# Two cross-attention layers on one core: layer 2's image scores taken from the bank of the row maxima instead of from a product of their own

## The chip, the cores and the metric

The kernel runs on one core of a Trainium2 chip. The metric is the device time of one execution in microseconds. A core has a matrix engine (TensorE; PE in the profile, with PEld for its weight loads), three engines for element work (VectorE = DVE, ScalarE = ACT, GpSimd = POOL) and a queue engine, SyncE (SP), which issues DMAs and does little else. Each engine runs its own instructions in order. SBUF is the on-chip memory of 128 partitions; PSUM is the small memory that matmuls write, used here in banks of 128 x 512 floats; DRAM lies off the engines and is reached by DMA alone.

## The reference

x is (16 images, 256 positions, 320 channels) and the context (16, 256 tokens, 512). Two layers run one after the other, each with 20 heads of width 16. What matters here is layer 2:

```python
q        = heads(x @ W_q)
k_t, v_t = heads(text @ W_k), heads(text @ W_v)      # text: first 252 tokens
probs_t  = softmax(q · k_t / 4)
text_out = probs_t @ v_t
k_ip, v_ip  = heads(ip @ W_k_ip), heads(ip @ W_v_ip) # ip: last 4 tokens, the "image tokens"
attn_scores = q · k_ip / 4                           # (b, 20 heads, 256, 4)
qsem  = l2norm(probs_t @ text);  sem = qsem · l2norm(ip)
probs_ip = softmax(attn_scores + 0.5 * sem) * spatial_mask
out = (text_out + probs_ip @ v_ip) @ W_out + b_out + x
```

All of it is float32. Layer 1 has the same build with 77 text tokens and 179 image tokens. The attn_scores line of layer 2 is what the change is about: each position has 20 x 4 = 80 of them.

## The kernel before, in words

**Precision.** TensorE multiplies rounded floats, so each operand is split into a rounded part and a rest, and `prod` (L198 to L206) multiplies the parts in three terms. A product of contraction depth 384 is so 9 matmuls, all on line L205.

**Slots.** Five groups of four heads make an image; 16 images make 80 slots a layer. `slot1(k)` (layer 2) is a list of steps written by hand. In slot k, `both1(k, t)` for the two halves t = 0, 1 of the positions makes the transposed scores of group k (L798, tile T) with their exponentials (ACT, L811), and the plain scores of group k+2 (L803, tile S: four heads of 256 columns in one tile of two PSUM banks, one buffer), whose row maxima VectorE takes with one `tensor_reduce` (L804). `maxima1` turns the maxima by matmul (L817), and a DMA puts them under the queries as one more contraction row. `attend1` (L848, L851) multiplies the probabilities with the values; `norm1` (L839, then VectorE's multiplication L840) makes the norm of qsem; `rounded1` (ACT L829, POOL L830) prepares it. `settle1` normalises with VectorE (L893, L896, L897).

**The columns of S.** The keys of an image are written to DRAM and read back in a stacked layout (`ks<-kd`). Keys are 256 columns: 252 text tokens and, from T1 = 252 on, the 4 image tokens' keys, which `keys1` copies in (L466). So each S tile already holds the four image scores of its heads in columns 252 to 255. The reduce L804 reads only the first 252.

**Image scores before.** `open1(b)` prepares image b: it loads x, makes the queries (`queries`, L551, with the splits ACT L559 and DVE L560), and then makes the image scores for itself: `image1` builds a masked key matrix with two VectorE multiplications of 128x384 (L529, from the constant `kmask`), nine matmuls multiply it with the queries (L205, `X<-q,kb`), and one VectorE transpose (L978) brings the result as `si` into the layout of the image softmax: partition 32s + r, eight blocks f, 32 columns, of which 20 (five groups by four tokens) are used. `image_softmax(b)` (L906 to L945) reads `si` on POOL about four slots after the scores were made; its line L945 multiplies the image values (`rs<-vipd`, loaded by SP) by `bmask`, a block mask of 128x384.

**What sets the order.** PE's instructions run in the program's order, pinned. Work besides the slots is in generator tasks (`k1` keys, `t1` tokens, `o1` open1, `i1` image softmax, `c1` close) with due times in slots, stepped by `fill`. `later(d, f)` runs f at d slots after now. In the main loop a scheduler of the framework orders the instructions of VectorE, ScalarE, GpSimd and SyncE; the order of each engine is then fixed in the program. All DMAs go through `dma` (L82) on SP, but for those of the maxima, which ScalarE issues. DMAs of SP rotate over eight completion counters ("lanes"), so that a DMA also waits for the one issued eight earlier. Tiles of one name rotate through a few buffers: three X banks, two T, one P, one S.

**The transition.** Layer 2's weights are split (`weights1`, `weights6`, `weights7`, `weights2`) and its first images opened during layer 1's last slots, at some 600 to 760 us of the profile. `bmask` is loaded at the first `settle1`.

Of the kernel before, what the change touches and what calls it, by code (L numbers as in the profile page):

```python
# [8 lines left out]
F32 = mybir.dt.float32  # L9
FR = mybir.dt.float32r  # L10
# [7 lines left out]
S = 256  # L18
# [3 lines left out]
CP = 384  # L22
E = 512
T0 = 77
NIP = 4
BI = B * NIP
T1 = S - NIP
# [3 lines left out]
NG = H // 4  # L31
# [6 lines left out]
NS = B * NG  # L38
# [10 lines left out]
def xattn2(  # L49
# [31 lines left out]
    def dma(out, in_):  # L81
        nc.sync.dma_start(*(f(ap) if ap.dtype == FR else ap for ap in (out, in_)))  # L82
# [6 lines left out]
    def bank(tag="X"):  # L89
        return ps.tile([128, 512], F32, tag=tag, name=tag, bufs=BANKS[tag])  # L90
# [25 lines left out]
    def const_tile(shape, tag, dtype=F32):  # L116
        return const.tile(shape, dtype, tag=tag, name=tag)
# [23 lines left out]
    def anchor(inst):  # L141
        anchors[inst.ins.engine] = inst
        return inst
# [140 lines left out]

    rn = const_tile([128, BI], "rn")
    kip = const_tile([128, 2, 3, BI], "kip", FR)
    kmask = const_tile([128, 3, 32], "kmask")


    def keys_out(d, m, kst, b=slice(None)):  # L290
# [80 lines left out]
    def weights1():  # L371


        cipn = buf("rawc", [128, 512], bufs=2, name="cipn")[:BI]
        dma(cipn, cip_d)
        yield
        sq = buf("rawc", [128, 512], bufs=2, name="sq")[:BI]
        nc.vector.tensor_mul(sq, cipn, cipn)
        nrm = rn[:BI, 0:1]
        nc.vector.tensor_reduce(nrm, sq, axis=AX.X, op=ALU.add)  # L380
        yield
        nc.scalar.activation(nrm, nrm, AF.Sqrt)
        yield
        nc.vector.tensor_scalar_max(nrm, nrm, 1e-12)
        nc.vector.reciprocal(nrm, nrm)
        dg = buf("rawc", [128, 512], bufs=2, name="dg")[:BI]
        nc.vector.memset(dg[:, BI : BI + 128], 1.0)
        nc.vector.tensor_scalar_mul(dg[:, :BI], ident[:BI, :BI], nrm)
        yield
        rp = bank()  # L390
        mm(rp[:, :BI], dg[:, BI : BI + 128], dg[:, :BI], start=True, stop=True)
        nc.vector.tensor_copy(rn, rp[:, :BI])
        cip = w1["cip"] = buf("kst", [128, 2, 4, BI], FR, bufs=SIZES["KST"], name="cip")
        raw = buf("rawc", [128, 4, BI], bufs=2, name="cipT")
        dma(raw, cipT_d.rearrange("(k p) n -> p k n", p=128))
        yield
        halves(cip[:, 0], cip[:, 1], raw, nc.vector, True)
        yield
# [11 lines left out]
    def weights6():  # L410
        cip = w1["cip"]
        wv = w1["wv"] = buf("wC", [128, 2, 4, H * D + NIP], FR)
        parts = [(wv1_d[k * 128 : (k + 1) * 128], wv[:, 0, k, : H * D], wv[:, 1, k, : H * D]) for k in range(4)]
        yield from in_turn(parts, 0.3, "rawc")
        wvi1 = yield from weights_by_column(wvi1_d, 0.3, "rawc")
        vip = buf("rawc", [128, 512], bufs=2, name="vip")[:BI, :CP]
        for m in range(3):
            ms = slice(m * 128, m * 128 + 128)
            vp = bank()[:BI, :128]
            prod(vp, lambda s, k: cip[:, s, k], lambda s, k: wvi1(s, k, ms), 4)  # L420
            nc.vector.tensor_copy(vip[:, ms], vp)
            yield
        ind1 = buf("M", [2, 2, S], FR, bufs=SIZES["M"], name="ind")
        nc.scalar.activation(ind1, ident[:2, :2].unsqueeze(2).to_broadcast([2, 2, S]), AF.Copy, scale=-1.0)
        w1["ind"] = ind1
        dma(kmask, kmask_d.rearrange("(m p) c -> p m c", p=128))
        dma(vipd, vip)
        for i in range(2):
            v = buf("wD", [128, 2, 640], bufs=2, name="v1t")
            nc.gpsimd.memset(v, 0.0)  # L430
            nc.vector.memset(vcols(v, V1W)[:, 0, :, 16], 1.0)
            nc.vector.tensor_scalar_add(vcols(v, V1W)[:, 1, :, 16], vcols(v, V1W)[:, 1, :, 16], tmask[:, 2:3])
            v1t.append(v)
        yield
# [44 lines left out]
    def tokens1(b):  # L479
# [41 lines left out]
                nc.vector.tensor_add(G[:, 5, :], g[:, S : S + 128], f(G[:, 5, :]))  # L521
            yield
        return V, G

    def image1(b):

        kb = buf("kb", [128, 2, 3, 32, NIP], FR)
        for s in range(2):
            nc.vector.tensor_mul(  # L529
                kb[:, s],  # L530
                f(kip[:, s, :, 4 * b : 4 * b + 4]).unsqueeze(2).to_broadcast([128, 3, 32, NIP]),
                kmask.unsqueeze(3).to_broadcast([128, 3, 32, NIP]),
            )
        return kb.rearrange("p s m c n -> p s m (c n)")

    def split(src, neg, eng, tag):

# [113 lines left out]
    def stacks1(k):  # L651
        b, g = divmod(k - NS, NG)
        n = 2 * SIZES["NR"]
        i = ((NS - SIZES["NR"]) % SIZES["NR"]) * 2 + (k - NS) % n
        Q, K = QK[k] = [x[i // 2 % SIZES["NR"]][:, 2 * (i % 2) : 2 * (i % 2) + 2] for x in (qs, ks)]
        get("k1", b)
        qd = get("o1", b)[0]
        for u in range(2):
            rows = slice(64 * u, 64 * u + XROW)
            hs = slice(4 * g + u, 4 * g + u + 3, 2)  # L660
            if k - NS < n:
                dma(K[64 * u + XROW : 64 * u + KS1], w1["ind"])
            dma(K[rows], stack_rows(kd[1][b][:, :, 0])[:, hs])
            dma(Q[rows], stack_rows(qd)[:, hs])
# [101 lines left out]
    def finish(l, b, hT, resid, extra=None):  # L766
# [14 lines left out]
        yield from project(l, wo[l], hh, evac)  # L781
        return y

    def both1(k, t, between=None):

        a = k + 2 < 2 * NS and QK[k + 2] 
        c = NS <= k < 2 * NS and QK[k]
        if a:
            if t == 0:
                maxes[k + 2] = buf("mn", [128, 4, 4], FR, bufs=2)[:, :2]  # L790
            sp = scores()
        if c:
            st = [bank("T").rearrange("p (h t) -> p h t", h=2) for u in range(2)]
            lo = (0, DUP)[t]
            for j in range(2):
                for u in range(2):
                    rows = slice(64 * u, 64 * u + KS1)
                    mm(st[u][:, j], c[1][rows, j, lo : lo + 128], c[0][rows, j], start=True, stop=True)  # L798
        if a:
            for j in range(2):  # L800
                for u in range(2):
                    rows = slice(64 * u, 64 * u + XROW)
                    mm(sp[:, 2 * u + j], a[0][rows, j, t * 128 : (t + 1) * 128], a[1][rows, j], start=True, stop=True)  # L803
            anchor(nc.vector.tensor_reduce(maxes[k + 2][:, t], sp[:, :, :T1], axis=AX.X, op=ALU.max))  # L804
        if between:
            between()
        if c:
            for u in range(2):
                if t == 0:
                    P[k, u] = buf("P", [128, 2, 2, S], bufs=SIZES["NP"])  # L810
                anchor(nc.scalar.activation(P[k, u][:, t], st[u], AF.Exp, scale=SCALE))  # L811
# [71 lines left out]
    def settle1(b, g, pv):  # L883
        hn = hsn
        if g == 0:
            norms[b] = buf("tmp", [128, NG, 8, 6], bufs=2, name="n1")
        nt = norms[b]
        if "na" not in w1:
            w1["na"], masks = [buf("nt", [128, 2, 8, 32], bufs=2, name="na") for i in range(2)]
            w1["bmask"] = masks.rearrange("p a f c -> p (a f c)")[:, :CP]  # L890
            dma(w1["bmask"], bmask_d)
        na = w1["na"][:, (NG * b + g) % 2]
        nc.vector.transpose(na.rearrange("p f c -> p (f c)"), pv[:, :S])  # L893
        nc.gpsimd.tensor_copy(nt[:, g], na[:, :, 16:22])
        rz = pv[:, S : S + 8]
        nc.vector.reciprocal(rz, na[:, :, 16])  # L896
        nc.vector.tensor_mul(  # L897
            hn[:, g // 2, :, g % 2], na[:, :, 0:16], rz.unsqueeze(2).to_broadcast([128, 8, 16])
        )
        if g == NG - 1:  # L900
            nc.gpsimd.tensor_copy(hn[:, 2, :, 1], hn[:, 2, :, 0])
            later(0.4, lambda: gather(1, b))

    def image_softmax(b, lo=0, hi=NG):

        gs, n = slice(lo, hi), hi - lo  # L906
        nt, si = norms[b][:, gs], get("o1", b)[1]
        pool = nc.gpsimd
        small = lambda n, t: buf(t, [128, NG, 8] + ([n] if n > 1 else []))[:, gs]

# [54 lines left out]
    def open1(b):  # L965
        x = load(x1d[b], "xq")
        yield
        xs = split(x, tmask[:, 5:6], nc.gpsimd, "hq")
        yield
        get("w2")  # L970
        qh, qd = yield from queries(1, xs)

        kb = image1(b)
        yield
        sp = bank()[:, :S]
        prod(sp, lambda s, k: kb[:, s, k], lambda s, k: qh[:, s, k], 3)
        si = buf("si", [128, 8, 32], bufs=3)
        nc.vector.transpose(si.rearrange("p f c -> p (f c)"), sp)  # L978
        yield
        return qd, si  # L980


    results, tasks, clock, delayed = {}, {}, [-99.0], []
# [17 lines left out]
    def get(*key):  # L1001
        while key not in results:
            step(key)
        return results[key]
# [5 lines left out]
    def later(slots, make):  # L1010
        delayed.append((clock[0] + slots, make))
# [196 lines left out]
```

## Time and profile before

| | |
|---|---|
| three runs, us | 1616.49, 1620.4, 1623.62 (median 1620.4) |
| the profiled execution, us | 1612.52 |
| its span in the trace, us | 1610.7 |
| mean granted TensorE clock | 0.977 |
| layer 2, one image in the steady stretch (1034.40 to 1088.70 us) | 54.30 us |

The profile is of one execution, 7.9 us under the median of the runs. It numbers time in us from the start of its span. "Busy" is the time that an engine had an instruction in flight; "idle before" in a row is the time the engine stood waiting ahead of that instruction, and the arrow names who released it. A row of a group gives line, engine, operation, tiles out and in, partitions x elements, count, busy time and mean ns of one.

### The profile page before, as it was taken

What the parts mean: (1) busy time and instruction counts of PE and PEld (TensorE: products, weight loads), DVE (VectorE), ACT (ScalarE), POOL (GpSimd) and SP (SyncE); (2) the same over time, 40 slices, a digit from 0 to 9 for tenths busy, and PEclk for the clock granted to TensorE, in tenths of its full rate; (3) what the DMA queues carried; (4) which work ended last, traced back from release to release, by engine and by line L of the source; (5) the groups of instructions that cost most, each with busy time, mean ns of one, the idle gap of its engine ahead of it and who ended that gap; (6) DMA issues with size and microseconds to landing.
All of it is one profiled execution on the core that took longest, in us unless ns stands there. A gap on an engine that the chain in (4) does not pass through costs nothing.

```text
span 1610.7 us, 36262 instructions
## 1 busy us (share of the span) xinstructions
PE 1518.9 (94%) x13194; PEld 1218.1 (76%) x13194; DVE 1212.2 (75%) x2426; ACT 847.1 (53%) x1861; POOL 1195.7 (74%) x1227
## 2 busy tenths in 40 slices
PE   7899999999999899789999999999999999999996
PEld 6787878787878787577777777777777777777765
DVE  5466777777777678877877787778777887788785
ACT  5344545555555545446656556555655655565562
POOL 3358787878787867777688768876877787778785
PEclk9899999999999899799999999999999999999998
DMA  6767777777677576665424333433343333423301
GB/s 218 214 200 204 206 204 206 205 205 211 199 204 210 170 213 174 162 198 177 149 67 133 114 127 96 131 119 120 96 136 121 107 109 127 130 90 104 110 27 45
DMA packets 235741, 243.05 MB, mean 151 GB/s; under 512 B 19050, under 2 KB 219468, under 8 KB 235564
## 3 DMA queue, kind: packets, MB, share of 16 engines
q1 hardware_dynamic: 233356, 239.44, 49.7%
q8 instruction: 105, 1.72, 0.4%
q10 hardware_dynamic: 2208, 1.30, 0.3%
q14 instruction: 72, 0.59, 0.1%
HBM read 116.78 MB, written 88.18 MB: 127 GB/s over the span
## 4 chain that ended last, share of the span: by engine, by line
PE 63%; DMA 9%; DVE 8%; POOL 8%; ACT 4%; issue 3%; SPq 1%; ACTq 0%; POOLq 0%; DVEq 0%
PE X L205 16%; PE X L839 13%; PE X L551 7%; PE P L732 6%; PE P L848 4%; PE S L675 4%; PE T L798 3%; PE P L851 3%; PE T L699 3%; POOL wt L830 2%; DMA kd<-kst 2%; DMA qs<-qd 2%; DMA qs<-mt 2%; PE S L803 2%; DVE wt L840 1%
## 5 line engine op out<-in xcount | busy, mean ns | idle before, releaser
L705 POOL TENSOR_TENSOR P<-P,rs 128x512 f32<-128x512 f32 x320 | 413.8, 1313 | 149.6 <-ACT P L702 149.5
L830 POOL TENSOR_TENSOR wt<-P,ctb 128x512 f32<-128x512 f32 x320 | 419.0, 1324 | 95.0 <-ACT ctb L829 93.6
L839 PE MATMUL X<-ctb,gm 128*128 128x512 f32 x1120 | 329.9, 412 | 0.7 <-DVE wt L840 0.4
L702 ACT ACTIVATE P<-T 128x512 f32<-128x512 f32 x320 | 176.0, 595 | 211.8 <-PE T L699 113.9
L839 PEld LDWEIGHTS X<-ctb,gm 128*128 128x128 f32 x1120 | 188.9, 188 | 69.2 <-issue 15.2
L840 DVE TENSOR_TENSOR wt<-X,wt 128x512 f32<-128x512 f32 x320 | 218.4, 683 | 18.9 <-PE X L839 13.4
L804 DVE TENSOR_REDUCE mn<-S 128x4 fp32r<-128x1008 f32 x160 | 191.7, 1198 | 49.1 <-PE S L803 48.9
L829 ACT ACTIVATE ctb<-P 128x512 fp32r<-128x512 f32 x320 | 195.1, 630 | 40.1 <-PE X L839 35.8
L811 ACT ACTIVATE P<-T 128x512 f32<-128x512 f32 x320 | 173.1, 593 | 68.9 <-PE P L848 53.8
L677 DVE TENSOR_REDUCE mn<-S 128x4 fp32r<-128x716 f32 x160 | 142.5, 891 | 0.0
L699 PE MATMUL T<-qs,ks 127*128 127x256 f32 x640 | 111.7, 294 | 21.9 <-DVE tmp L749 9.8
L732 PE MATMUL P<-P,vr 128*32 128x256 f32 x1920 | 128.7, 404 | 0.9 <-DVE mx L604 0.9
L675 PE MATMUL S<-ks,qs 125*128 125x256 f32 x640 | 118.4, 309 | 4.9 <-DVE mn L677 2.8
L675 PEld LDWEIGHTS S<-ks,qs 125*128 125x128 f32 x640 | 89.2, 196 | 41.3 <-issue 36.2
L551 PE MATMUL X<-ho,wF 128*128 128x256 f32 x768 | 113.2, 291 | 6.5 <-DVE ho L541 3.0
L551 PE MATMUL X<-hq,wE 128*128 128x256 f32 x768 | 109.7, 286 | 7.1 <-ACT hq L540 3.2
L917 POOL TENSOR_TENSOR r<-u,rs 128x40 f32<-128x40 f32 (+2 forms) x17 | 108.7, 6394 | 7.4 <-DVE u L914 7.2
L551 PEld LDWEIGHTS X<-ho,wF 128*128 128x128 f32 x768 | 103.7, 195 | 12.7 <-DVE ho L541 4.6
L699 PEld LDWEIGHTS T<-qs,ks 127*128 127x128 f32 x640 | 92.5, 197 | 27.2 <-DVE tmp L749 11.2
L551 PEld LDWEIGHTS X<-hq,wE 128*128 128x128 f32 x768 | 102.3, 193 | 11.3 <-ACT hq L540 3.7
L205 PE MATMUL X<-cta,wA 128*128 128x252 f32 (+1 forms) x720 | 101.1, 287 | 8.9 <-ACT wA L147 5.8
L205 PEld LDWEIGHTS X<-cta,wA 128*128 128x128 f32 x720 | 94.3, 193 | 15.1 <-ACT wA L147 6.1
(207 smaller groups left out, 2854.9 us busy)
## 6 DMA issues: line engine op xcount, KB each, us to landing
qd<-q SPq DMA_DIRECT2D x96, 384.0 KB
qs<-tph SPq DMA_DIRECT2D x64, 308.0 KB
kd<-kst SPq DMA_DIRECT2D x73, 256.0 KB
rawc<-in_cT_dram SPq DMA_DIRECT2D x60, 256.0 KB
qs<-qd SPq DMA_DIRECT2D x80, 192.0 KB
ks<-kd SPq DMA_DIRECT2D x80, 192.0 KB
ks<-kd SPq DMA_DIRECT2D x160, 96.0 KB
qs<-qd SPq DMA_DIRECT2D x160, 96.0 KB
```

The lines of the kernel that those rows point to most:

```text
L205: last = mm(out, lhs(a, k), rhs(b, k), start=i == 0, stop=i == len(terms) - 1)
L551: mm(pp, w(s, k, slice(m * 128, (m + 1) * 128)), a[:, t], start=i == 0, stop=i == len(terms) - 1)
L675: mm(sp[:, h], Q[: XROW + T0, h, t * 128 : (t + 1) * 128], K[: XROW + T0, h], start=True, stop=True)
L699: mm(st[p][:, j], K[:KS0, 2 * p + j, t * 128 : (t + 1) * 128], Q[:KS0, 2 * p + j], start=True, stop=True)
L702: exp = anchor(nc.scalar.activation(pt, st[p], AF.Exp, scale=SCALE))
L705: anchor(nc.gpsimd.tensor_mul(pt, pt, rs[:, t : t + 1].to_broadcast([128, 2, S])))
L732: mm(pv[32 * s : 32 * s + 32, o : o + S], v[:, vt, h : h + 32], P[k, s // 2][:, t, s % 2], start=vt < 2, stop=vt != 1,)
L804: anchor(nc.vector.tensor_reduce(maxes[k + 2][:, t], sp[:, :, :T1], axis=AX.X, op=ALU.max))
L829: nc.scalar.activation(R[k, u][:, t], P[k, u][:, t], AF.Copy, scale=0.5)
L830: anchor(nc.gpsimd.tensor_sub(W[k, u][:, t], P[k, u][:, t], f(R[k, u][:, t])))
L839: mm(yp, gm[:, gb], R[k, u][:, kt], start=i == 0, stop=i == len(blocks[n]) - 1)
L840: nc.vector.tensor_mul(W[k, u][:, n], yp, W[k, u][:, n])
```

## The change

Layer 2's image scores are no longer computed by a product of their own. Behind each row maximum (L804) VectorE copies columns 252 to 255 of the same S tile, for four heads, into a tile `sq` of SBUF. After an image's last half, `sq` goes to DRAM (`sd`), and 0.6 slots later eight DMAs read it back into `si` in the softmax's layout, in pieces of 20 floats. `si` has 20 columns instead of 32. The key matrix `image1`, its constant `kmask`, its nine matmuls and the transpose go. `bmask` is copied DRAM to DRAM (`hop`) where the first weights of layer 2 are emitted and loaded from there into the buffers that `image1` used; it is no longer loaded at the first `settle1`. In the order of SP's program, the copy to `hop` stands where `kmask` was loaded, as the 19th DMA of the kernel.

```diff
-    kmask = const_tile([128, 3, 32], "kmask")
...
         dma(cipn, cip_d)
+        hop = w1["hop"] = dram.tile([128, CP], F32, name="hop")
+        dma(hop, bmask_d)
...
-        dma(kmask, kmask_d.rearrange("(m p) c -> p m c", p=128))
+        w1["bmask"] = f(buf("kb", [128, CP], FR, name="bmask"))
+        dma(w1["bmask"], w1["hop"])
...
-    def image1(b):
-
-        kb = buf("kb", [128, 2, 3, 32, NIP], FR)
-        for s in range(2):
-            nc.vector.tensor_mul(
-                kb[:, s],
-                f(kip[:, s, :, 4 * b : 4 * b + 4]).unsqueeze(2).to_broadcast([128, 3, 32, NIP]),
-                kmask.unsqueeze(3).to_broadcast([128, 3, 32, NIP]),
-            )
-        return kb.rearrange("p s m c n -> p s m (c n)")
...
+    def image_scores(k, t, sp):
+
+        b, g = divmod(k - NS, NG)
+        if (g, t) == (0, 0):
+            image[b] = buf("sq", [128, 2, 4, NG * NIP], bufs=2)
+        sq = image[b]
+        nc.vector.tensor_copy(sq[:, t, :, NIP * g : NIP * (g + 1)], sp[:, :, T1:S])
+        if (g, t) == (NG - 1, 1):
+            sd = dram.tile([128, 2, 4, NG * NIP], F32, tag="sd", name="sd", bufs=2)
+            dma(sd, sq)
+            later(0.6, lambda: image_out(b, sd))
+
+    def image_out(b, sd):
+
+        si = image[b] = buf("si", [128, 8, NG * NIP], bufs=3)
+        for s in range(4):
+            for u in range(2):
+                dma(si[32 * s : 32 * s + 32, 4 * u : 4 * u + 4], sd[:, u, 2 * (s % 2) + s // 2].rearrange("(a r) x -> r a x", r=32))
...
             anchor(nc.vector.tensor_reduce(maxes[k + 2][:, t], sp[:, :, :T1], axis=AX.X, op=ALU.max))
+            image_scores(k + 2, t, sp)
...
-            w1["na"], masks = [buf("nt", [128, 2, 8, 32], bufs=2, name="na") for i in range(2)]
-            w1["bmask"] = masks.rearrange("p a f c -> p (a f c)")[:, :CP]
-            dma(w1["bmask"], bmask_d)
+            w1["na"] = buf("nt", [128, 2, 8, 32], bufs=2, name="na")
...
-        nt, si = norms[b][:, gs], get("o1", b)[1]
+        nt, si = norms[b][:, gs], image[b]
...
-        kb = image1(b)
-        yield
-        sp = bank()[:, :S]
-        prod(sp, lambda s, k: kb[:, s, k], lambda s, k: qh[:, s, k], 3)
-        si = buf("si", [128, 8, 32], bufs=3)
-        nc.vector.transpose(si.rearrange("p f c -> p (f c)"), sp)
-        yield
-        return qd, si
+        return qd
```

More of the change, by code (lines that the diff above doesn't have):

```diff
@@ L656, in stacks1 @@
         get("k1", b)
-        qd = get("o1", b)[0]
+        qd = get("o1", b)
         for u in range(2):
@@ L782, in finish @@
         return y
+    image = {}
+    def image_scores(k, t, sp):
[13 more added lines that the diff above has]
+                dma(si[32 * s : 32 * s + 32, 4 * u : 4 * u + 4], sd[:, u, 2 * (s % 2) + s // 2].rearrange("(a r) x -> r a x", r=32))
     def both1(k, t, between=None):
```

## The prediction, on record before the changed kernel ran

> **What bounds the kernel now.** I read the page's busy line and chain first, then the table by windows, then what PE waited for, and only then single instructions.
>
> ```profile
> span 1610.7 us, 36262 instructions
> ...
> PE 1518.9 (94%) x13194; PEld 1218.1 (76%) x13194; DVE 1212.2 (75%) x2426; ACT 847.1 (53%) x1861; POOL 1195.7 (74%) x1227
> ...
> PE 63%; DMA 9%; DVE 8%; POOL 8%; ACT 4%; issue 3%; SPq 1%; ACTq 0%; POOLq 0%; DVEq 0%
> ```
>
> The averages hide stages. The table by windows has, after the stretch and its length: busy us (count) of PE, PEld, DVE, ACT and POOL, the granted clock, the DMA share and GB/s.
>
> ```profile
> 640.00:700.00 60.00, 45.07 (x395) 34.62 (x395) 47.27 (x96) 28.02 (x63) 43.84 (x45) 0.83 0.67 181
> 700.00:755.00 55.00, 48.42 (x432) 40.17 (x433) 42.07 (x78) 29.43 (x65) 43.50 (x51) 1.00 0.61 188
> ...
> 1034.40:1088.70 54.30, 53.63 (x461) 41.13 (x460) 43.02 (x80) 30.80 (x67) 41.29 (x45) 1.00 0.36 117
> 1088.70:1143.10 54.40, 53.70 (x462) 41.09 (x460) 43.09 (x80) 30.95 (x68) 41.47 (x45) 1.00 0.38 117
> ```
>
> The last two rows are two images of layer 2's steady stretch: PE is busy in 53.6 of 54.3 us, idle in 0.7; DVE has 11.3 us free, POOL 13. So there a matmul less is time less, unless something else comes late; and a small operation more on DVE costs only where PE waits for DVE. The first two rows are the transition: PE is idle in 14.9 + 6.6 = 21.5 us, DVE often the cause. PE's waits over six steady images (us in total, times, longest):
>
> ```profile
> PE X L954 <- DVE wt L840: 2.5, 6, 0.4
> PE X L520 <- DVE gm L516: 1.1, 6, 0.2
> ```
>
> Two waits an image, both on DVE, 0.4 and 0.2 us. These are the places to which new DVE work can reach.
>
> **Term 1: the product goes.** The timeline of PE around one image's product, and the same place in a slot without one; first its group over the whole trace:
>
> ```profile
> L205 PE MATMUL X<-q,kb 128*128 128x256 f32 x144 | 20.8, 288 | 0.2
> ```
> ```profile
> 1044.62 0.70 PE L954 MATMUL X<-rs,rs 128*128 128x256 f32 x2 [0.43 <-DVE wt L840]
> ...
> 1045.85 0.28 PE L817 MATMUL X<-ident_r,mn 128*4 128x128 f32 x2
> 1046.06 0.50 PE L798 MATMUL T<-qs,ks 50*128 50x256 f32 x4
> ...
> 1067.34 0.28 PE L817 MATMUL X<-ident_r,mn 128*4 128x128 f32 x2
> 1067.46 1.27 PE L205 MATMUL X<-q,kb 128*128 128x256 f32 x9
> 1068.66 0.51 PE L798 MATMUL T<-qs,ks 50*128 50x256 f32 x4
> ```
>
> From L817 to L798 it takes 1068.66 - 1067.34 = 1.32 us with the product and 1046.06 - 1045.85 = 0.21 without: 1.11 us an image, with no idle before any of the three. The program order of the changed kernel has the same PE instructions without these 144, so 16 x 1.11 = **-17.8 us**. The two images whose product lies in the transition, where PE has idle time anyway, may give less; the range takes that in.
>
> **Term 2: the copies.** Ten per image, 160 in all, each 128x16 from PSUM. In the changed program each stands directly behind its reduce on DVE. No such copy is in the trace. The nearest rows in size, with the two operations that go:
>
> ```profile
> L529 DVE TENSOR_TENSOR kb<-kip,kmask 128x384 fp32r<-128x384 f32 x32 | 35.6, 1115 | 5.9 <-PE X L205 5.9
> ...
> L746 DVE RECIPROCAL P<-nt 128x16 f32<-128x16 f32 x80 | 19.7, 246 | 0.0
> ...
> L747 DVE TENSOR_TENSOR P<-P,mk 128x8 f32<-128x8 f32 x80 | 13.4, 168 | 1.6
> L978 DVE STREAM_TRANSPOSE si<-X 128x256 f32<-128x256 f32 x16 | 7.0, 437 | 0.5 <-PE X L205 0.5
> ```
>
> 0.17 us (8 elements) and 0.25 us (16, a reciprocal) bound it; I take 0.2, between. Ten are 2.0 us an image, and 2 x 1.115 + 0.437 = 2.67 us go, so DVE's load falls by 0.7 us an image. The sum isn't the point, though: the removed work stood in one place, the new is spread over ten. Which of the ten can PE feel? The one in the chain to the 0.43 us wait, on DVE:
>
> ```profile
> 1041.87 0.65 DVE L840 TENSOR_TENSOR wt<-X,wt 128x512 f32<-128x512 f32 x1
> 1042.44 0.41 DVE L560 TENSOR_TENSOR q<-X,q 128x256 fp32r<-128x256 f32 x1
> 1042.78 1.19 DVE L804 TENSOR_REDUCE mn<-S 128x4 fp32r<-128x1008 f32 x1
> 1043.89 0.67 DVE L840 TENSOR_TENSOR wt<-X,wt 128x512 f32<-128x512 f32 x1
> ```
>
> DVE works without a gap from 1041.87 to 1044.56, and PE's L954 starts at 1044.62, when this L840 has freed its bank. A copy behind the reduce of 1042.78 makes L954 late by its whole length: 0.2 us. Queued behind it on DVE are L840 and L955, behind L954 on PE everything. The other nine stand before gaps of DVE's or on banks that PE needs later; the only other wait in the list, L516's, has one more reduce ahead. For the nine together I take 0.1 (bounds 0 and 1.8). So +0.3 us an image; with 14 images in the steady stretch **+4.2 us** (bounds 0 and 28).
>
> In a sentence of its own: the Trainium skill, "VectorE: DVE Perf Modes", section "The TRN2 errata — SBUF-src ops pay a fixed extra latency per instruction", gives a VectorE operation from PSUM 120 cycles plus one per element at 0.96 GHz, and warns that many small tiles pay the fixed part each, which speaks against ten small copies; the estimate by it is 136 / 0.96 = 142 ns, and term 2 would be 3.0 us. The trace agrees on the reduce (1128 cycles are 1.175 us, the row has 1.19), and no run here shows a copy yet.
>
> The S tile is freed later by the copy too. It is a single buffer, so the next L803 waits for it. Of the ten in the image of 1034 us, the tightest pair is a reduce on DVE and the next L803 on PE:
>
> ```profile
> 1049.10 1.20 DVE L804 TENSOR_REDUCE mn<-S 128x4 fp32r<-128x1008 f32 x1
> ```
> ```profile
> 1052.19 0.40 PE L803 MATMUL S<-ks,qs 48*128 48x256 f32 x4
> ```
>
> 1052.19 - 1050.30 = 1.89 us are free, nine copies long. Cost nothing; if that cover were gone, 0.2 us for each slot half.
>
> **Term 3: the way through DRAM.** Nine DMAs an image on SP. The timeline of SP, and the last reduce of the image on DVE:
>
> ```profile
> 1079.57 0.43 SPq L82 DMA_DIRECT2D qs<-qd  x1
> 1091.34 0.39 SPq L82 DMA_DIRECT2D out_dram<-xc  x1
> 1095.06 0.38 SPq L82 DMA_DIRECT2D xc<-x1d  x1
> ...
> 1096.06 0.44 SPq L82 DMA_DIRECT2D rawc<-in_cT_dram  x1
> 1099.76 0.53 SPq L82 DMA_DIRECT2D rs<-vipd  x1
> ```
> ```profile
> 1086.38 1.20 DVE L804 TENSOR_REDUCE mn<-S 128x4 fp32r<-128x1008 f32 x1
> ```
>
> SP stands idle from 1080.0 to 1091.3. The last copy ends at about 1086.38 + 1.20 + 0.2 = 1087.8, so sd is issued then, in the gap. The first si waits at SP's head until sd has landed: at most 3.7 us, what xc, which needs out_dram's transfer done, waited behind it (1091.34 to 1095.06). The new order is sd, four si, out_dram, two si, xq, si, xc, si, rawc, rs. At some 0.48 us an issue out_dram goes at 1093.4 at the latest, xc 3.7 us behind it at 1097.1, rawc at about 1098.1. rs waits for PE until 1099.76 in any case: 1.2 us of margin. And si is read by POOL some four slots later, 40 us. So **0**. If the cover were gone, rs is what is late, and VectorE's L945 with it (the third rival).
>
> **Term 4: the transition.** On the chain of waits, on PE and on DVE there stand:
>
> ```profile
> 641.59 1.36 DVE kb L529 x2
> ```
> ```profile
> 753.65 0.22 PE L817 MATMUL X<-ident_r,mn 128*4 128x128 f32 x1 [0.85 <-DVE mn L804]
> ```
> ```profile
> 756.46 0.94 DVE L945 TENSOR_TENSOR rs<-rs,nt 128x384 f32<-128x384 f32 x1 [1.68 <-DMA nt<-in_bmask_dram]
> ```
>
> The L529 at 641.59 is in the chain that ended last: up to -1.36. PE's 0.85 is a reduce that DVE comes to late, after two L529; with the early bmask L945's 1.68 us of idle go as well, but no PE wait hangs on those in the rows. Other products of this stretch give a little. Late next is the split of weights on the same engine. I take **-3** (bounds -8 and +2: new copies, and 18 DMAs more for the first two images on a crowded SP).
>
> **Term 5: the start.** kmask goes, hop comes at its place among the first loads:
>
> ```profile
> 12.10 0.43 SPq L82 DMA_DIRECT2D kmask<-in_kmask_dram  x1
> ```
> ```profile
> GB/s 218 214 200 204 206 204 206 205 205 211 199 204 210 170 213 174 162 198 177 149 67 133 114 127 96 131 119 120 96 136 121 107 109 127 130 90 104 110 27 45
> ```
>
> 192 KB instead of 48 KB; 144 KB at the first slice's 218 GB/s are 0.7 us, twice that if read and write both count, nothing if the loads behind it aren't late. I take **+0.4** (0 to 1.4).
>
> **The sum.** -17.8 + 4.2 + 0 - 3 + 0.4 = -16.2 us. Against the profiled execution, 1612.5 us (span 1610.7 and 1.8 around it), that is 1596.3. That execution is 7.9 us below the median of the runs, 1620.4; against the median the forecast is 1620.4 - 16.2 = **1604**.
>
> **The rivals.**
> *Bigger gain.* No copy is felt and the transition gives 8: -17.8 - 8 = -25.8, 1595. For it: DVE has less to do in sum. Against: the L954 chain above has no gap.
> *The copies eat the gain.* DVE works in order, and PE at 99% has no idle time to take up delays. If half of the ten copies are felt, 1.0 us an image in place of 0.3, the loss is 0.7 x 14 = 9.8: 1614, within what counts as no change; if all ten, 1.7 x 14 = 23.8: 1628. Break-even is at about seven of ten. Against it stand the 1.89 us on the S tile and the two short waits.
> *rs comes late: slower.* It is one mechanism: SP issues in order and the nine DMAs stand ahead of rs<-vipd. The price can be read one image earlier, on SP and on DVE:
>
> ```profile
> 1045.35 0.53 SPq L82 DMA_DIRECT2D rs<-vipd  x1
> ```
> ```profile
> 1050.21 0.80 DVE L945 TENSOR_TENSOR rs<-rs,nt 128x384 f32<-128x384 f32 x1
> ```
>
> L945 comes 4.9 us after the issue, without a wait. If rs is issued late by more than this leaves, DVE stands there, behind it the L840 that frees PE's banks, and each us is a us of PE. It decides from about 1.2 us of such lateness an image (16.2 / 14); at 3 us the loss is 42, 1646; at 2 us, 28, **1632**. For it speaks that one si is 128 pieces of 80 bytes, and that with eight lanes a slow si holds up what is issued eight later: rawc waits for the fourth si. Against it: the margin of 1.2 us by upper bounds, and 5 us between that si and rawc. By the Trainium skill, "DMA: Bandwidth & Descriptors", section "Specifications", a transfer needs 512 B for line rate; 80 B are below it, which makes this rival likelier; no run here shows such an si yet.
> *It isn't what it says.* Were copies moved away from their reduces, the S tile would be held; the program order shows none moved.
>
> **How the numbers follow.** About 0.5%, 8 us, is what a measurement of this kernel can tell from no change; the borders are 1612 and 1628. The forecast and its near surroundings (1595 to 1612) get 0.63, the bigger gain beyond that 0.08, the eaten gain 0.15, the late rs 0.14. The first two are faster, 0.71; the third is the same, 0.15; the fourth slower, 0.14. The range of 1593 to 1618 holds the first, most of the second and the milder half of the eaten gain, about 0.8.
>
> **What would show each step.** Right: in the steady windows an image of about 53.5 us (54.35 - 1.11 + 0.3), PE idle about 1.0 us of it; a copy row of 0.14 to 0.25 us; PE's wait at L954 about 0.6 us; S waits none; sd issued in SP's gap, rs right after PE's L954; no idle of DVE ahead of L945. Wrong: a new PE wait S L803 <- DVE of the copy; PE waits at L839 or L798 that weren't there; L945 with "<-DMA rs" before it; an image of 54 us or more.

## The result, and the profile after

The changed kernel runs in 1594.39 us (median of four, 1590.43 to 1596.61) against 1618.7 us (median of four) for the kernel before: ratio 0.9849, 95% interval 0.9829 to 0.9869. That is 24 us less; 16 were forecast (1604), and the time lies within the stated range of 1593 to 1618, near its lower end. Its profiled execution took 1596.61 us, 15.9 less than the profiled one of before. Which of the two differences is the change's will have to be settled first.

Line numbers move in the changed kernel: L810 and L815 are the old L798 and L803 (T and S scores), L816 the reduce, L783 the new copy, L830 the old L817, L852/L853 the norm's L839/L840, L965 the old L954, L956 the old L945, L518/L522 the old L516/L520, and L690, L723 and L740 the old L699, L732 and L749. In the other kernels below they move again; the text names the old line beside the new one. The page:

```profile
span 1594.8 us, 36348 instructions
...
PE 1507.8 (95%) x13050; PEld 1206.7 (76%) x13050; DVE 1192.8 (75%) x2538; ACT 848.6 (53%) x1861; POOL 1192.1 (75%) x1227
...
PE 67%; DMA 8%; DVE 8%; POOL 6%; ACT 4%; issue 3%; SPq 2%; ACTq 0%; POOLq 0%; DVEq 0%
```

PE has 144 matmuls less; DVE has 112 instructions more (160 copies, 48 gone) and yet is busy 19 us less. The table by windows, in the transition and in one steady image (columns as in the prediction):

```profile
640.00:700.00 60.00, 46.82 (x408) 36.03 (x408) 48.41 (x99) 28.71 (x64) 46.45 (x49) 0.84 0.77 209
700.00:755.00 55.00, 50.57 (x416) 41.11 (x417) 38.27 (x77) 29.40 (x65) 41.07 (x48) 0.92 0.56 171
...
1019.80:1073.30 53.50, 52.72 (x457) 40.16 (x457) 41.38 (x86) 31.01 (x66) 41.40 (x45) 1.00 0.39 121
```

In the steady window DVE is busy 41.4 us where it was 43.0. The length of an image is read from one matmul that comes once in each, the last pair of L954 (now L965). In the kernel before, on PE, nine images apart:

```profile
935.93 0.70 PE L954 MATMUL X<-rs,rs 128*128 128x256 f32 x2 [0.41 <-DVE wt L840]
```
```profile
1424.98 0.70 PE L954 MATMUL X<-rs,rs 128*128 128x256 f32 x2 [0.40 <-DVE wt L840]
```

and in the changed one, the same nine images:

```profile
931.86 0.70 PE L965 MATMUL X<-rs,rs 128*128 128x256 f32 x2 [0.54 <-DVE wt L853]
```
```profile
1411.89 0.70 PE L965 MATMUL X<-rs,rs 128*128 128x256 f32 x2 [0.54 <-DVE wt L853]
```

489.05 / 9 = 54.34 us before, 480.03 / 9 = 53.34 after: **1.00 us an image**. PE's waits over six images of the changed kernel are the same two, and the first has grown:

```profile
PE X L965 <- DVE wt L853: 3.3, 6, 0.6
PE X L522 <- DVE gm L518: 1.1, 6, 0.2
```

The copy's group, and then the chain to that wait on DVE's timeline:

```profile
L783 DVE COPY sq<-S 128x16 f32<-128x16 f32 x160 | 25.9, 162 | 0.0
```
```profile
1089.90 1.19 DVE L816 TENSOR_REDUCE mn<-S 128x4 fp32r<-128x1008 f32 x1
1091.02 0.16 DVE L783 COPY sq<-S 128x16 f32<-128x16 f32 x1
1091.10 0.67 DVE L853 TENSOR_TENSOR wt<-X,wt 128x512 f32<-128x512 f32 x1
```

A copy is 162 ns long, but the next instruction starts 80 ns after it: the row's duration overlaps its neighbour's. On SP's timeline the way through DRAM:

```profile
1080.37 0.34 SPq L82 DMA_DIRECT2D sd<-sq  x1
1081.98 1.73 SPq L82 DMA_DIRECT2D si<-sd  x4
...
1088.68 0.39 SPq L82 DMA_DIRECT2D rawc<-in_cT_dram  x1
1092.56 0.53 SPq L82 DMA_DIRECT2D rs<-vipd  x1
```

sd has landed at the latest 1.6 us after its issue (the first si goes out then); rawc's issue is done at 1089.1, and rs goes out another 3.5 us later, 0.73 us after the start of PE's L965 at 1091.83. Lastly the transition, before on DVE and on PE, then after on both:

```profile
641.50 2.35 DVE L529 TENSOR_TENSOR kb<-kip,kmask 128x384 fp32r<-128x384 f32 x2
...
644.24 1.45 DVE L148 TENSOR_TENSOR wC<-rawc,wC 128x320 fp32r<-128x320 f32 x1
...
646.71 0.41 DVE L749 TENSOR_TENSOR tmp<-nt,P 128x256 f32<-128x256 f32 x1
```
```profile
647.17 0.80 PE L699 MATMUL T<-qs,ks 127*128 127x256 f32 x2 [3.87 <-DVE tmp L749]
```
```profile
643.60 0.42 DVE L740 TENSOR_TENSOR tmp<-nt,P 128x256 f32<-128x256 f32 x1
```
```profile
644.18 1.05 PE L690 MATMUL T<-qs,ks 127*128 127x256 f32 x4
```

Before, the pair L529 stood ahead of L749, which by the row releases the last two of PE's four L699 and L732 behind them; a cast of 1.45 us stood between as well, and PE waited 3.87 us. After, L740 (the old L749) stands ahead of that cast, and PE's four L690 run without a break.

### The profile page after: what moved, and what is told of

It is laid out like the page before. It is cut to its first block, busy times and chain, and to the rows that moved or that the text cites. A ratio compares the mean times of both kernels' runs of the same rounds, so it can differ in the third digit from the quotient of the medians.

```text
span 1594.8 us, 36348 instructions
## 1 busy us (share of the span) xinstructions
PE 1507.8 (95%) x13050; PEld 1206.7 (76%) x13050; DVE 1192.8 (75%) x2538; ACT 848.6 (53%) x1861; POOL 1192.1 (75%) x1227
## 4 chain that ended last, share of the span: by engine, by line
PE 67%; DMA 8%; DVE 8%; POOL 6%; ACT 4%; issue 3%; SPq 2%; ACTq 0%; POOLq 0%; DVEq 0%
PE X L205 16%; PE X L852 14%; PE X L542 7%; PE P L723 6%; PE P L861 4%; PE S L666 4%; PE T L810 4%; PE P L864 4%; PE T L690 3%; DMA qs<-qd 2%; DMA kd<-kst 2%; POOL wt L843 2%; PE S L815 2%; SPq L82 2%; DMA qs<-mt 1%
## 5 line engine op out<-in xcount | busy, mean ns | idle before, releaser
L852 PE MATMUL X<-ctb,gm 128*128 128x512 f32 x1120 | 330.0, 412 | 0.5 <-DVE wt L853 0.3
L852 PEld LDWEIGHTS X<-ctb,gm 128*128 128x128 f32 x1120 | 189.1, 188 | 68.1 <-issue 21.4
L853 DVE TENSOR_TENSOR wt<-X,wt 128x512 f32<-128x512 f32 x320 | 218.2, 683 | 20.8 <-PE X L852 12.7
L842 ACT ACTIVATE ctb<-P 128x512 fp32r<-128x512 f32 x320 | 195.1, 630 | 41.4 <-PE X L852 38.5
L816 DVE TENSOR_REDUCE mn<-S 128x4 fp32r<-128x1008 f32 x160 | 191.7, 1198 | 25.7 <-PE S L815 25.0
L723 PE MATMUL P<-P,vr 128*32 128x256 f32 x1920 | 132.2, 411 | 1.7 <-DVE mx L595 1.6
L690 PE MATMUL T<-qs,ks 127*128 127x256 f32 x640 | 110.9, 294 | 18.1 <-DMA qs<-mt 9.1
L690 PEld LDWEIGHTS T<-qs,ks 127*128 127x128 f32 x640 | 92.0, 197 | 22.9 <-DVE tmp L740 7.3
```

What stands on the lines that cost most here:

```text
L690: mm(st[p][:, j], K[:KS0, 2 * p + j, t * 128 : (t + 1) * 128], Q[:KS0, 2 * p + j], start=True, stop=True)
L723: mm(pv[32 * s : 32 * s + 32, o : o + S], v[:, vt, h : h + 32], P[k, s // 2][:, t, s % 2], start=vt < 2, stop=vt != 1,)
L842: nc.scalar.activation(R[k, u][:, t], P[k, u][:, t], AF.Copy, scale=0.5)
L852: mm(yp, gm[:, gb], R[k, u][:, kt], start=i == 0, stop=i == len(blocks[n]) - 1)
L853: nc.vector.tensor_mul(W[k, u][:, n], yp, W[k, u][:, n])
```

## The experiments

The theory after the first result: PE's 1.11 us an image are the gain; one copy in ten is felt; in the transition the pair of multiplications of image 0 costs PE more than itself. The rivals: copies that pile up, an SP queue that makes rs late, and a gain that comes from the mask's new place. And first, whether 24 or 16 us are to be explained.

**How far do executions of one program differ?** `before_again` is the kernel before, `after_again` the changed one, both unchanged.

> The kernel before, unchanged, against itself, for what differs between executions of one program. The changed kernel's trace is 15.9 us shorter in its span, its median 24.3 us; layer 1, whose instructions are the same, drifts by -3.9 to +1.9 us between the two traces. Theory 'scatter' (the change is worth about 16 us and the rest is chance of execution): ratio 1.000 within 0.003, and a second profile whose layer 1 (100 to 640 us) differs from the first by several us. Theory 'the change is worth 24 us': the ratio is 1.000 as well, but the profiles of both kernels, taken again, lie about 24 us apart.

> The changed kernel, unchanged, timed in five rounds. Theory 'PE work less the exposed copy' (16 x 1.11 us less, some 0.15 us an image more, some us in the transition): ratio 0.988 to 0.991 (about 15 to 19 us). Theory 'worth 24 us': 0.985 or less, and the profile has places outside the steady images of layer 2 where some 8 us go.

The kernel before against itself: 1.0001 (0.9987 to 1.0015). The changed one: 0.986 (0.9841 to 0.9878), that is 20 to 26 us less. The second profile of the kernel before has a span of 1621.7 us, 11 more than the first, without one instruction changed. The table by windows of its two profiles, first and second, shows where:

```profile
100.00:640.00 540.00, 512.09 (x4706) 439.38 (x4706) 398.17 (x894) 270.42 (x626) 428.62 (x408) 0.98 0.69 199
640.00:760.00 120.00, 98.49 (x881) 78.35 (x882) 92.64 (x179) 59.07 (x131) 89.33 (x97) 0.91 0.64 184
```
```profile
100.00:640.00 540.00, 514.53 (x4675) 441.94 (x4677) 397.31 (x889) 270.95 (x624) 426.34 (x407) 0.97 0.68 197
640.00:760.00 120.00, 96.11 (x839) 75.36 (x832) 87.53 (x168) 53.67 (x121) 86.51 (x94) 0.89 0.61 174
```

The granted clock (the third number from the end) is 0.01 to 0.02 lower there, and fewer matmuls fit into the same stretch. So the first profile of before was a lucky execution: the 15.9 us between the two profiles understate the change, and the 24 of the first medians lie within the second interval too. Steady images, at a clock of 1.00, don't have this scatter: the same nine images of the second profile take 54.35 us each.

**The product, and the copies by themselves.** `no_product` leaves out layer 2's image scores (the softmax reads zeros) with all that made them; `copies_only` keeps the old path and adds the 160 copies, whose tile nobody reads.

```diff
 no_product
+        w1["si"] = buf("si", [128, 8, 32], bufs=1)
+        nc.gpsimd.memset(w1["si"], 0.0)
...
-        kb = image1(b)
         yield
-        sp = bank()[:, :S]
-        prod(sp, lambda s, k: kb[:, s, k], lambda s, k: qh[:, s, k], 3)
-        si = buf("si", [128, 8, 32], bufs=3)
-        nc.vector.transpose(si.rearrange("p f c -> p (f c)"), sp)
+        si = w1["si"]
 copies_only
+    def image_scores(sp):
+
+        nc.vector.tensor_copy(buf("sq", [128, 4, NIP], bufs=2), sp[:, :, T1:S])
...
             anchor(nc.vector.tensor_reduce(maxes[k + 2][:, t], sp[:, :, :T1], axis=AX.X, op=ALU.max))
+            image_scores(sp)
```

> Left out: the image scores of layer 2 (the softmax reads zeros); no key matrix, no product, no transpose, no copies, no DMAs for them; the block mask is loaded late as before. Theory 'the product's PE time is the gain': 16 x 1.11 = 17.8 us and up to 3 in the transition, ratio 0.987 to 0.989; it beats the changed kernel by the exposed copies alone, 2 us. Rival 'a good part of the gain is the early block mask or the transition': this kernel gains 8 us less than the changed one.

> The old path is kept whole; behind each row maximum the copy of the four columns is added, into a small tile that nobody reads (no DMAs). Theory 'one copy in ten is felt': 0.13 to 0.2 us an image, 2 to 3 us in all, ratio 1.001 to 1.002; PE's wait at L954 grows from 0.42 to about 0.55 us, no new wait at S. Rival 'the copies eat': half of the ten are felt, 0.8 us an image, 12 us, ratio 1.007 to 1.008; all ten, 26 us, 1.016.

`copies_only`: 1.0027 (1.001 to 1.0043), between the two theories. Its steady images tell them apart; on PE, eleven images apart:

```profile
863.57 1.27 PE L205 MATMUL X<-q,kb 128*128 128x256 f32 x9
```
```profile
1462.27 1.28 PE L205 MATMUL X<-q,kb 128*128 128x256 f32 x9
```

598.70 / 11 = 54.43 us, 0.09 more than before, at a granted clock of 1.00. So ten copies cost about 0.1 us an image here; half of them felt would be 0.4 by the measured 80 ns. The rest of the 0.27%, some 3 us, isn't in the steady images, and where it is wasn't found.

`no_product`: 0.9895 (0.9877 to 0.9913), 17 us less, *fewer* than the changed kernel. That spoke for the rival that the early mask brings the rest.

**Is it the mask?** `bmask_late` is the changed kernel with the mask loaded at the first settle1 and no hop; `no_product_early` is `no_product` with hop and the early mask, without kmask.

```diff
 bmask_late
-        hop = w1["hop"] = dram.tile([128, CP], F32, name="hop")
-        dma(hop, bmask_d)
...
-        w1["bmask"] = f(buf("kb", [128, CP], FR, name="bmask"))
-        dma(w1["bmask"], w1["hop"])
...
-            w1["na"] = buf("nt", [128, 2, 8, 32], bufs=2, name="na")
+            w1["na"], masks = [buf("nt", [128, 2, 8, 32], bufs=2, name="na") for i in range(2)]
+            w1["bmask"] = masks.rearrange("p a f c -> p (a f c)")[:, :CP]
+            dma(w1["bmask"], bmask_d)
```

> The changed kernel with the block mask loaded late again, at the first settle1, and no copy to DRAM at the start. Theory 'the early mask is worth nothing, or costs 0.4 us': same as the changed kernel, ratio 0.985 to 0.987. Rival 'the rest of the gain is the early mask' (the kernel without product, mask late, gained 17 us, the changed one 23, and its trace is about 5 us behind in the transition): ratio 0.989 to 0.990, and the stretch of 625 to 765 us is some 5 us longer than in the changed kernel.

> Left out: the image scores of layer 2, as before, but the block mask is loaded early as in the changed kernel and kmask is gone. Rival 'the early mask is worth some 6 us': ratio 0.984 to 0.985, 2 us better than the changed kernel. Theory 'the mask is worth nothing': 0.989 to 0.990 as with the late mask.

`bmask_late` 0.9835 (0.9808 to 0.9862), `no_product_early` 0.9835 (0.9805 to 0.9866); both medians, 1594.48 and 1595.02, are the changed kernel's. The mask's new place is worth nothing measurable to the changed kernel, and the rival falls. Why `no_product` alone gained 17 can be read in part from its trace: in the transition it has two PE waits, of 2.68 and 2.46 us, that `no_product_early` hasn't. The second hangs on the late mask, on DVE and PE (L947, L806 and L819 are the old L945, L804 and L817):

```profile
756.61 0.81 DVE L947 TENSOR_TENSOR rs<-rs,nt 128x384 f32<-128x384 f32 x1 [1.87 <-DMA nt<-in_bmask_dram]
757.34 1.20 DVE L806 TENSOR_REDUCE mn<-S 128x4 fp32r<-128x1008 f32 x1
```
```profile
758.59 0.22 PE L819 MATMUL X<-ident_r,mn 128*4 128x128 f32 x1 [2.46 <-DVE mn L806]
```

VectorE's order in this kernel has the product with the mask ahead of a row maximum that PE needs; in the kernel before and in `bmask_late` it stands behind that maximum, and the mask's lateness doesn't reach PE. So a late mask costs where the order puts it ahead of such work. The first wait, for a cast of ScalarE's, and the rest of the difference stay open. The image without product or copies, from `no_product_early`, the same nine images on PE (L945 and L833 are the old L954 and L840):

```profile
931.80 0.70 PE L945 MATMUL X<-rs,rs 128*128 128x256 f32 x2 [0.41 <-DVE wt L833]
```
```profile
1410.53 0.70 PE L945 MATMUL X<-rs,rs 128*128 128x256 f32 x2 [0.40 <-DVE wt L833]
```

478.73 / 9 = 53.19 us: the product, with its work on VectorE, is worth 54.34 - 53.19 = 1.15 us an image, and the copies of the changed kernel cost 53.34 - 53.19 = 0.15. Of this the longer wait at L965 is 0.13 (3.3 us in place of 2.5 over six images).

**Twice the copies.** `copies_twice` adds a second copy of the same columns behind each first.

```diff
         nc.vector.tensor_copy(sq[:, t, :, NIP * g : NIP * (g + 1)], sp[:, :, T1:S])
+        nc.vector.tensor_copy(buf("sq2", [128, 4, NIP], bufs=2), sp[:, :, T1:S])
```

> The changed kernel with a second copy of the same columns behind each first, into a tile that nobody reads. The first copy costs 0.12 to 0.15 us an image (trace: 1.11 - 1.0). Theory 'one copy in ten is felt': another 0.15 us an image, 2 to 2.5 us in all, ratio to the kernel before up by 0.001 to 0.002; PE's wait at L965 grows by one copy, to 0.7 us. Rival 'the copies begin to pile up': over 0.6 us an image more, 9 us.

0.9888 (0.9859 to 0.9916), 7 us more than the changed kernel, and 0.71 us an image ((1468.68 - 874.17) / 11 = 54.05, from the two rows below) where 0.15 was expected: the rival's number. But it isn't ten copies adding up. PE's waits, and the first and last L966 (the changed kernel's L965):

```profile
PE X L522 <- DVE gm L518: 6.7, 6, 1.1
PE X L966 <- DVE wt L854: 2.0, 6, 0.3
```
```profile
874.17 0.70 PE L966 MATMUL X<-rs,rs 128*128 128x256 f32 x2 [0.33 <-DVE wt L854]
```
```profile
1468.68 0.70 PE L966 MATMUL X<-rs,rs 128*128 128x256 f32 x2 [0.33 <-DVE wt L854]
```

L966 waits even less, by 0.2 us; what grew is one wait, at L522, from 0.2 to 1.1 us. The two together make the 0.71. DVE and POOL ahead of L518, from one timeline of both:

```profile
1078.35 0.68 DVE L854 TENSOR_TENSOR wt<-X,wt 128x512 f32<-128x512 f32 x1
...
1078.95 1.57 DVE L533 SCALAR_TENSOR_TENSOR hq<-hq,tmask,xq 128x256 fp32r<-128x256 f32 x1
1078.95 3.94 POOL L844 TENSOR_TENSOR wt<-P,ctb 128x512 f32<-128x512 f32 x3
```

and the same place in the changed kernel:

```profile
1080.86 0.47 DVE L533 SCALAR_TENSOR_TENSOR hq<-hq,tmask,xq 128x256 fp32r<-128x256 f32 x1
1081.15 1.34 POOL L843 TENSOR_TENSOR wt<-P,ctb 128x512 f32<-128x512 f32 x1 [0.72 <-ACT ctb L842]
```

The scheduler, with the longer VectorE program, has changed the order around L533, which now starts together with a POOL operation and takes 1.57 us; in the changed kernel it starts while POOL stands idle and takes 0.47. The group rows over six images, changed kernel and `copies_twice`:

```profile
L533 DVE SCALAR_TENSOR_TENSOR hq<-hq,tmask,xq 128x256 fp32r<-128x256 f32 x6 | 2.8, 473 | 0.0
```
```profile
L533 DVE SCALAR_TENSOR_TENSOR hq<-hq,tmask,xq 128x256 fp32r<-128x256 f32 x6 | 9.5, 1576 | 0.0
```

The added copies change the order, and L533 takes 1.1 us more in the new one, ahead of the L518 that PE waits for. This is read from the traces; no run has the second copies in the old order. By the Trainium skill, "SBUF — State Buffer", section "Who interferes with whom", a VectorE instruction with two SBUF inputs contends with a GpSimd instruction that reads SBUF, and the one that comes second waits for the other's end; the trace agrees, the 1.1 us more being nearly one POOL operation (1.3).

**The way through DRAM.** `si_twice` and `si_thrice` issue each load of si two and three times.

```diff
             for u in range(2):
+                for _ in range(2):
                     dma(si[32 * s : 32 * s + 32, 4 * u : 4 * u + 4], sd[:, u, 2 * (s % 2) + s // 2].rearrange("(a r) x -> r a x", r=32))
```

> The changed kernel with each of the eight loads of si issued twice on SP, so that eight more DMAs of 128 pieces of 80 bytes stand ahead of rs<-vipd in each image. Theory 'the way through DRAM is hidden': at 0.45 us an issue 3.6 us more on SP; if the margin ahead of rs is about 1 to 4 us, the steady image stays within 0.1 us, at most L945's row gets a short wait. Rival 'SP's queue is near its limit': rs lands some 2 us late, L945's row of VectorE shows a wait for it and the image grows by up to 2 us, ratio 1.00.

> The changed kernel with each of the eight loads of si issued three times: 16 more DMAs an image ahead of rs<-vipd. With each issued twice rs went out 1.95 us after the PE matmul it waits for, in place of 0.73, and L945 of the kernel before (rs times the mask, on VectorE) still started 5.6 us after that matmul, as in the changed kernel: the slack took it. Eight more issues at 0.57 us make rs 4.5 us later still, issued 6.5 us after the matmul; with some 2 to 3 us to land it comes at 8.5 to 9.5. Theory 'rs late stalls VectorE and PE': L945 shows a wait of 3 to 4 us an image, the image grows by 2.5 to 3.5 us, 35 to 50 us in all, ratio 1.007 to 1.017. Rival 'nothing hangs on it': the steady image stays within 0.2 us of the changed kernel's, and the slower way that the prediction named was never near.

0.9832 (0.9805 to 0.9858) and 0.9841 (0.9813 to 0.9869): nothing. In `si_twice` the margin is used up, as SP's and PE's timelines show:

```profile
1082.08 5.10 SPq L82 DMA_DIRECT2D si<-sd  x9
1087.28 0.39 SPq L82 DMA_DIRECT2D rawc<-in_cT_dram  x1
1087.77 1.13 SPq L82 DMA_DIRECT2D rs<-vipd  x1
```
```profile
1085.82 0.70 PE L966 MATMUL X<-rs,rs 128*128 128x256 f32 x2 [0.56 <-DVE wt L854]
```

rs follows rawc without a pause, 1.95 us after the matmul instead of 0.73, but VectorE's product with it still starts 5.6 us after that matmul (at 1091.42), as in the changed kernel (1097.42, matmul at 1091.83). In `si_thrice` the scheduler put rs ahead of the last seven si, so rs wasn't later still; the point from which a late rs costs was not reached by either run, and its price wasn't measured.

**The transition.** `keys_first` is the changed kernel with the two multiplications of image 0 alone kept, unread, with kmask's load and the late mask.

```diff
...
         qh, qd = yield from queries(1, xs)
 
+        if b == 0:
+            image1(b)
+        yield
         return qd
```

> The changed kernel with the two multiplications of 128x384 kept for image 0 alone (their result is not read), kmask loaded at its old place and the block mask loaded late. In the kernel before, this pair stands on VectorE at 641.5 us ahead of the operation that frees PE's bank, and PE waits 3.87 us there; in all kernels without it the stretch of 635 to 645 us is 3.6 to 5.3 us shorter. Theory 'the pair makes that wait': PE's wait of about 4 us is back at the same place, 2.4 us of DVE costing more than themselves since a cast behind them slows as well; 625 to 765 us longer by some 4 us, ratio up by 0.0025. Rival 'the order around it has changed anyway': no such wait, ratio as the changed kernel's. And the first 300 us, shorter by 1 to 3 us in kernels without kmask: longer again if kmask's load is the cause, not if chance of the clock is.

0.9903 (0.9882 to 0.9924), 1602.28 us, some 8 us above `bmask_late`. PE's wait is back where it was (L699 and L749 have the same numbers here as in the kernel before):

```profile
649.56 0.80 PE L699 MATMUL T<-qs,ks 127*128 127x256 f32 x2 [4.10 <-DVE tmp L749]
```

Matched instruction by instruction with the first profile of before, PE's stretch from 635 to 645 us is 3.6 to 5.3 us shorter in the kernels without the pair (4.65 in the changed kernel's first profile) and 0.6 shorter in this one, about what the second profile of before shows too (0.7); its steady images are the changed kernel's. So two instructions of 1.2 us each on VectorE, in one place, cost PE about 4 us. That is half of the 8 us; the other half isn't shown. Over the first 300 us, matched in the same way, the five kernels with kmask's load lie 0 to 1.9 us above that first profile, this one 0.2, and the nine without it from 3.7 below to 1.5 above; the means are 0.9 above and 1.3 below. The two overlap, the granted clock scatters there, and no run takes kmask's load alone away: what kmask and hop do at the start stays open.

One more wait of the transition is gone, the 0.85 us ahead of L817 at 753.65 that the prediction lists. In the changed kernel, on PE:

```profile
752.70 0.28 PE L830 MATMUL X<-ident_r,mn 128*4 128x128 f32 x2
```

Matched in the same way, the stretch from 750 to 755 us is 1.07 us shorter in every kernel without the product, `keys_first` among them, but for `no_product` with its wait for the mask, and the same within 0.1 us in the second profile of before and in `copies_only`.

**Can the felt copy be moved?** `copy_behind_norm` orders each copy behind the next norm multiplication; `copies_act` puts it on ScalarE.

```diff
 copy_behind_norm
-            image_scores(k + 2, t, sp)
+            pending.append((k + 2, t, sp))
...
-        nc.vector.tensor_mul(W[k, u][:, n], yp, W[k, u][:, n])
+        flush(nc.vector.tensor_mul(W[k, u][:, n], yp, W[k, u][:, n]))
 copies_act
-        nc.vector.tensor_copy(sq[:, t, :, NIP * g : NIP * (g + 1)], sp[:, :, T1:S])
+        nc.scalar.copy(sq[:, t, :, NIP * g : NIP * (g + 1)], sp[:, :, T1:S])
```

> The changed kernel with each copy ordered on VectorE behind the next multiplication L840 of the kernel before (it frees the bank PE waits for), not directly behind its reduce. Theory 'the felt copy is the one in the chain to L954': PE's wait there is 0.42 us again in place of 0.55, the steady image some 0.12 us shorter, 2 us in all, ratio 0.001 below the changed kernel. Rival 'the S tile is then held too long': the reduce's tile is held about 0.7 us longer of 1.9 free; PE waits at S, the image gets longer.

> The changed kernel with the ten copies of an image on ScalarE. ScalarE is busy in 31 of 54 us an image and holds the exponentials and the casts that PE's operands come from. Theory 'only the chain on VectorE feels a copy': 0.12 us an image less, ratio 0.001 below the changed kernel. Rival 'a copy in ScalarE's order waits for the S tile ahead of exponentials, or they for it': PE waits at T or at the ScalarE casts appear, ratio above the changed kernel by 0.003 or more.

`copy_behind_norm`: 0.9907 (0.9882 to 0.9931), 8 us worse than the changed kernel; my theory lost to the rival. The wait at L954 is gone, and one at S has come, 0.6 us an image. On PE, and on DVE just before it (L825 makes S, L966 is the old L945, L863 the norm's L840):

```profile
884.89 0.51 PE L825 MATMUL S<-ks,qs 48*128 48x256 f32 x4 [0.67 <-DVE P L917]
```
```profile
882.60 0.80 DVE L966 TENSOR_TENSOR rs<-rs,kb 128x384 f32<-128x384 f32 x1
...
884.59 0.15 DVE L783 COPY sq<-S 128x16 f32<-128x16 f32 x1
```

Between a reduce and the next norm there may stand three other operations, here L966 and two transposes; the copy ran 1.99 us after L966 had started, and S was free only at 884.74. PE's row names L917, the instruction behind the copy, but L917 doesn't touch S; the one that frees S is the copy. It is the very place, the reduce with the old L945 behind it, whose 1.89 us the prediction called free.

`copies_act`: 0.9856 (0.9835 to 0.9877), 1594.03 us. PE's waits over six images, and the copy on ScalarE:

```profile
PE X L965 <- DVE wt L853: 2.5, 6, 0.4
PE X L522 <- DVE gm L518: 1.0, 6, 0.2
```
```profile
L783 ACT COPY sq<-S 128x16 f32<-128x16 f32 x60 | 10.6, 176 | 11.2 <-DVE mn L816 11.1
```

The wait is 0.4 us again, and the image, (1410.08 - 931.45) / 9 = 53.18 us by the same matmul, is as short as without copies. That is 0.16 us an image, some 2 in all, less than these times can tell: it beats the kernel before as the changed one does, and it isn't shown to beat the changed one.

## Why the prediction was right, and where its sizes were off

- **The bound.** Right: PE bounds the steady images, at a clock of 1.00, and its waits stayed the two named.
- **Term 1, the product.** Forecast 1.11 us an image, measured 1.15 (`no_product_early`). 16 x 1.15 = 18.4; the two products in the transition count too: matched with the first profile of before, the stretch around the second, 740 to 745 us, is 0.94 us shorter.
- **Term 2, the copies.** The mechanism was right (the copy in the chain to L954, wait 0.42 to 0.54), the size off: forecast +0.3 us an image, measured +0.15, so 14 x 0.15 = 2.1 us in place of 4.2. The copy's row is 0.162 us long, just under the lower bound of 0.17, and it delays its successor by 0.08; the prediction took the whole length for the delay. The page's figure by the Trainium skill, "VectorE: DVE Perf Modes", section "The TRN2 errata — SBUF-src ops pay a fixed extra latency per instruction", 0.142 us, is nearer to the row's 0.162 than my 0.2; neither is the 0.08 by which the copy lengthens the chain.
- **The S tile.** Right that it costs nothing behind the reduce; but the 1.89 us were no general margin: `copy_behind_norm` used them up with instructions that stand there anyway.
- **Term 3, DRAM.** Right, 0. The margin was 3.5 us, not the 1.2 worked out from the 3.7 us that a 384 KB store takes; sd, of 80 KB, lands within 1.6.
- **Term 4, the transition.** The largest miss: forecast -3, of which up to 1.36 for the pair at 641.59 because that is its piece of the chain of waits. PE's wait behind it was 3.87 us, and it went whole; `keys_first` brought a wait of 4.1 back. The row was in PE's waits of that stretch, and the step that failed is taking the pair's own time for its price: behind it in VectorE's order stood both parts of a row maximum (L676, L677), the slow cast and L600, ahead of the L749 that PE waited for; without the pair it stands ahead of all of them. With this the pair is worth some -4.5 (3.6 to 5.3) in place of -1.36. The reading of the 0.85 us wait as a reduce that VectorE comes to late fits the traces: it went, worth -1.1. The rest of the transition doesn't stand out from the scatter.
- **Term 5, the start.** +0.4 was not seen; by the means of the profiles the start is shorter by some 2 us, not longer, but they overlap, and the sign stays open.
- **The sum.** -18.4 + 2.1 - 4.5 - 1.1 = -21.9 us, within both intervals (0.9841 to 0.9878 is 20 to 26 us less, 0.9829 to 0.9869 is 21 to 28). The forecast's 16 was short by the transition (2.6) and the copies (2.1). The some 2 us between the sum and the medians' 24 aren't accounted for.
- **Against which time.** Profile against profile gives 15.9, nearly my 16.2, and is chance: the first profile of before was 11 us shorter in span than its second.
- **The rivals.** The eaten gain: no, 0.15 us an image, of the 0.8 by which ten copies delay their successors; yet one more copy each, with the order that followed, cost 0.71 an image. The late rs: not near. The bigger gain (1595): the result, 1594.4, lies just beyond its border, to which the prediction gave a chance of 0.08, but not by its mechanism: a copy is felt, and the transition gave 5.6, not 8. That the time lies inside the range, 1.4 us above its lower end, is in part luck.

## What to carry to other kernels

Work taken off the engine that is 99% busy comes back whole (1.15 us an image, 1.11 forecast), if the added work stands in the order where another engine's wait isn't; look for the one chain that ends in a wait and count only what stands in it. What an instruction costs in a stage full of waits is not its own time but the wait that ends behind it: read the waits of that stretch one by one, and follow the queue back from each. And compare profiles only where the granted clock is the same.

## What the runs showed of the hardware

- The same VectorE instruction (128x256, two SBUF inputs) took 0.473 or 1.576 us, as GpSimd stood idle at its start or an operation of GpSimd's started with it.
- A copy of 128x16 from PSUM: 0.162 us on VectorE and 0.176 on ScalarE; on VectorE the next instruction starts 0.08 us after it.
- 24 DMAs of 80-byte pieces an image on SP, in place of eight, changed no image's length.
- Two executions of one program differed by 11 us in span, with granted clocks of 0.98 and 0.97 from 100 to 640 us and 0.91 and 0.89 from 640 to 760.
